# Feed-forward outputs by feature with scale and bias on ScalarE, and two chunk sums on TensorE in every second block

## The chip, the cores and the metric

The kernel runs on one core of a Trainium2 chip. The metric is the device time in microseconds (us), the median of several executions. Five engines work side by side, each through its own queue in program order: TensorE (PE; its weight loads are shown apart as PEld), VectorE (DVE), ScalarE (ACT), GpSimd (POOL) and SyncE (SP), which issues most transfers. TensorE writes its results into PSUM, used here as eight banks of 128 partitions by 512 float32 numbers.

## The reference

```python
# x: (4, 2048, 512); 16 heads of 32; w = sign(weights), +1 or -1
q, k, v = (x @ W.T split into heads for W in (Wq, Wk, Wv))
attn = softmax(q @ k.T / sqrt(32))          # over all 2048 keys
x = layernorm(x + attn @ v)
y = clip((x @ w.T) * scale + bias, -100, 100)   # scale, bias: one per output feature
x = layernorm(x + y)
```

## The kernel before

There are 4 batches. The 16 heads are taken in 4 head groups of 4 heads (`NG = HG = 4`), so there are 16 passes `n` (batch `n // 4`, group `n % 4`). A pass has 4 query blocks `qb` of 512 queries, and a block has 16 key chunks `kc` of 128 keys. A step `s` is one chunk of one block: 64 steps (`STEPS`) to a pass and 1024 in all.

In every step TensorE computes `scores` (L323): four small bf16 matmuls (L327) that add the negated row maxima, then four matmuls of 32 rows each (L333) into four banks. ScalarE turns these into exponentials `p` (L340). `max_unit` (L264) computes scores a second time for a step some 22 ahead, in the other orientation (L275), into four more banks; VectorE takes the row maximum of three of them (L282), ScalarE copies the fourth to SBUF (`moved`, L294) and VectorE reads it there. In every even step `weighted` (L344) multiplies two chunks of `p` with the values (L351), and VectorE adds the result to `oT` (L363). `max_parts` collects a block's maxima once per block.

The sums over `p` are needed as softmax denominators. GpSimd adds the chunks of a block into `acc` (`add_up`, L372, the add is L377); `chunks_added` says how many chunks go there. The chunks from there on are kept in `last_p`, and `denominators` (L400) sums them and `acc` over the keys on TensorE with a matrix of ones (`ones_times`, L381 to L385). `ppool` has five buffers for `p`.

Everything else is put between as tasks: projections of k and q (256 columns each, `project_k`, `project_q`), of v (128 columns, `project_v`), all through `piece` (L229, matmuls L233, ScalarE copy L237), transposes of the input (`transpose_x`, L214), `add_attention` (L460), and the `Finish` of a finished block of rows. A planner (`plan`, L762) decides in which step each goes. A task has a kind ("col", "small" or "big"), a first and a last step, and may wait for another task. In the middle of the program "col" goes into even steps and "small" and "big" into odd steps, one small as a rule and at most two units of big work; `weight` (L759) gives a k or q projection two units. A first plan counts the units of each pass, and the second spreads them by this quota. A step with `add_attention` or with `max_parts` in it is called heavy. Fillers are emitted after the step's scores and row-maximum matmuls and before `weighted`. Calls put into `behind[s]` with `at` are emitted at the end of step `s`.

PSUM banks are handed out by `take` (L83): the bank that a simple model of the engines' times expects free first. `runs`, `spend` and `give` only keep that model. All eight banks are in use by the scores and row maxima of every step.

`Finish` (L481) handles 512 rows of a batch when their attention is complete: `load`, first `stats`, `rstd` (a power on GpSimd, L524), `shift` and `norm` (ScalarE, L542); then per tile `j` of 128 rows `turn` (L548: four transposes L552, `high` on ScalarE L557, the remainder `low` on VectorE L559; both parts are read by matmuls of one pass) and `ffn` (L563) in two halves of 256 output columns. A half is eight matmuls (L570) with a row tile's part as the stationary operand and the sign weights moving, so that rows stand on the partitions, followed by four VectorE operations: times scale (L575), plus bias (L576), clip (L577), all in place in PSUM, and the sum with the row in SBUF (L579). Scale and bias are broadcast to 128 partitions at the start (L180, L181). Then second `stats`, `rstd`, `shift`, `norm` and `store`. `finish` (L611) lays these out for batches 0 to 2, during the passes of the next batch, one block per 64 steps (54 in the last); `finish_last` for the last batch's first three blocks; `finish_end` for its last block, after the last step (`total`), tile by tile.

Of the kernel before, what the change touches and what calls it, by code (L numbers as in the profile page):

```python
# [21 lines left out]
def kernel(  # L22
# [28 lines left out]
    HALF = D // 2  # L51
# [18 lines left out]
    work = ctx.enter_context(tc.tile_pool(name="work", bufs=2))  # L70
# [89 lines left out]
    scale_bc = const.tile([P, D], F32, name="scale_bc")  # L160
    bias_bc = const.tile([P, D], F32, name="bias_bc")

    def load_first():

        first = ppool.tile([P, DC, D], F32, tag="p", name="first_w")
        for i, name in enumerate(("wk", "wq", "wv")):
            xin[name, 0] = first[:, i, :]
        for name in ("wk", "wq"):
            nc.scalar.dma_start(out=xin[name, 0], in_=rows_of[name][ds(0, P), :])
        for g in range(NQB):  # L170
            t = ppool.tile([P, NTQ, D], F32, tag="p", name="first_x")
            for j in range(NTQ):
                xin[0, g, j] = t[:, j, :]
                nc.sync.dma_start(out=t[:, j, :], in_=x[0, ds(g * QB + j * P, P), :])

    def load_rest():
        nc.scalar.dma_start(out=xin["wv", 0], in_=wv[ds(0, P), :])
        raws["ws"] = xpool.tile([P, DC, D], F32, tag="xg", name="raw_ws")
        nc.scalar.dma_start(out=raws["ws"], in_=w_ffn.rearrange("(c p) i -> p c i", p=P))
        nc.sync.dma_start(out=scale_bc, in_=ffn_scale.partition_broadcast(P))  # L180
        nc.sync.dma_start(out=bias_bc, in_=ffn_bias.partition_broadcast(P))  # L181
# [184 lines left out]
    def chunks_added(n, qb):  # L366

        if is_last(n, qb):
            return NT // 2
        return NT - 1  # L370
# [108 lines left out]
    shared = []  # L479

    class Finish:  # L481
        def __init__(self, b, g):
            self.b, self.g = b, g
            self.mv, self.rs, self.nb, self.nT, self.rows_rs = {}, {}, {}, {}, {}
            self.room = None
# [62 lines left out]
        def turn(self, j):  # L548
# [6 lines left out]
            high = work.tile([P, DC, P], F32R, tag="high", name="high")  # L555
            low = work.tile([P, DC, P], F32R, tag="low", name="low")
# [4 lines left out]
            self.nT[j] = high, low  # L561

        def ffn(self, j, half):  # L563
            cols = slice(0, D) if half is None else ts(half, HALF)
            wide = D if half is None else HALF
            i = take()
            py = ps[:, i, :wide]
            for k, part in enumerate(self.nT[j]):
                for c in range(DC):
                    nc.tensor.matmul(  # L570
                        py, lhsT=part[:, c, :], rhs=wT["ws"][:, c, cols],
                        start=(k == c == 0), stop=(k == 1 and c == DC - 1),
                    )
            runs("full", 3.4e-3 * wide)
            nc.vector.tensor_tensor(py, py, scale_bc[:, cols], ALU.mult)  # L575
            nc.vector.tensor_tensor(py, py, bias_bc[:, cols], ALU.add)  # L576
            nc.vector.tensor_scalar(py, py, MAX_VAL, -MAX_VAL, ALU.min, ALU.max)  # L577
            dst = self.row(j)[:, cols]
            nc.vector.tensor_tensor(dst, dst, py, ALU.add)  # L579
            give(i, "DVE", 0.6 + 4.2e-3 * wide)  # L580
# [30 lines left out]
    def finish(b, qb, a, every, w, lag):  # L611
        f = Finish(b, qb)
        at(a, f.load)
        for j in range(NTQ):
            at(a + 2 + j, f.stats, 1, j)
        at(a + 6, f.rstd, 1)
        at(a + 7 + lag, f.shift, 1)
        for j in range(NTQ):
            t = a + 8 + lag + every * j
            at(t, f.norm, 1, j)  # L620
            turned = task("small", t + 1, t + 3, f.turn, j)
            for k in range(2):
                task("big", t + 2, t + w, f.ffn, j, k, after=turned)
            at(t + w, f.stats, 2, j)
        e = a + 9 + lag + every * (NTQ - 1) + w
        at(e, f.rstd, 2)
        at(e + 1 + lag, f.shift, 2)
        for j in range(NTQ):
            at(e + 2 + lag + j, f.norm, 2, j)
        at(e + 5 + lag, f.store)  # L630

    def finish_last(qb, last):
# [9 lines left out]
        for j in range(NTQ):  # L642
            t = a + 5 + (j if late else 3 * j)
            by = t + 6
            at(t, f.norm, 1, j)
            if late:
                by = total + (-1, 1, 4, 5)[j]
            turned = task("small", t + 1, t + 3, f.turn, j)
            for k in [None] if late else range(2):
                task("big", by if late else t + 2, by, f.ffn, j, k, after=turned)  # L650
            at(by + late, f.stats, 2, j)
        e = total + 7 if late else a + 21
# [6 lines left out]
    def finish_end(qb, last):  # L659
# [10 lines left out]
        for j in range(NTQ):  # L670
            t = total + (6, 6, 7, 8)[j]
            turned = task("small", t, t, f.turn, j)
            t = total + 7 + j
            task("big", t, t, f.ffn, j, None, after=turned)
            at(t, f.stats, 2, j)
            at(t, f.rstd, 2, j, j + 1)
            at(t + 1, f.shift, 2, j, j + 1)
            at(t + 1, f.norm, 2, j)
            at(t + 1, f.store_tile, j)
# [16 lines left out]
    for n in range(N):  # L696
# [32 lines left out]
        for qb in range(NQB):  # L729
# [12 lines left out]
            if g == NG - 1:  # L742
                if b < B - 1:
                    every = 13 if b < B - 2 else 11
                    finish(b, qb, (b + 1) * NG * STEPS + qb * (5 * every - 1), every, every, 3)
                else:
                    (finish_end if is_last(n, qb) else finish_last)(qb, last)
# [8 lines left out]
    def on_vector(t):  # L756
        return t[3].__name__ == "ffn"

    def weight(t):  # L759
        return 2 if t[3] in (project_k, project_q) else 1  # L760

    def plan(quota=None):  # L762
# [9 lines left out]
        while any(len(gone[kind]) < len(tasks[kind]) for kind in tasks):  # L772
# [10 lines left out]
            for kind in most:  # L783
# [8 lines left out]
                if kind == "big":  # L792
                    if middle and quota is not None and not heavy:
                        k = max(1, min(k, -(-quota[group] * (at_n + 1) // STEPS) - used[group]))


                    thirds = [t for t in can if on_vector(t)]
                    values = [t for t in can if t[3] is project_v]
                    wide = [t for t in can if weight(t) == 2]
                    if heavy or any(map(on_vector, must)):  # L800
                        thirds = []
                    k -= sum(map(weight, must))
                    if k < 1:
                        can = []
                    elif must:
                        can = values[:1] or thirds[:1]
                    elif k == 1:
                        can = values[:1] or thirds[:1] or wide[:1]
                    elif thirds and values:
                        can = thirds[:1] + values[:1]  # L810
                    else:
                        can = wide[:1] or values[:2] or thirds[:1]
                else:
                    can = can[: max(0, k - len(must))]
                picked = must + can
                for t in sorted(picked, key=lambda t: not on_vector(t)):
# [94 lines left out]
```

## Time and profile before

| | |
|---|---|
| median of 3 runs | 4385.39 us (4384.27 to 4385.4) |
| profiled execution, its time | 4384.56 us |
| profiled execution, its span | 4382.7 us, granted clock 0.996 |
| PE, PEld busy | 4331.6, 2081.3 us |
| DVE, ACT, POOL busy | 3381.3, 2994.6, 4083.0 us |
| chain of work that ended last | PE 94%, DVE 2%, POOL 2%, ACT 2% |

The span runs from the first to the last instruction; the time also holds what lies around it. Busy times overlap, since the engines work side by side. A busy PE can still wait: matmuls are pipelined, and a group of four that starts together and has one member waiting is shown as busy throughout. So for PE the distance from the start of one group to the start of the next says more than its busy time.

### The profile page before, as it was taken

The numbers are of one execution on the slowest core, as the hardware profiler recorded it, in microseconds if no ns is written. First come the engines' busy times: TensorE is split into PE (matmuls) and PEld (weight loads), VectorE is DVE, ScalarE is ACT, GpSimd is POOL, SyncE is SP. The second block draws the span as 40 slices with busy tenths as digits, with TensorE's granted clock in tenths as the row PEclk, the third lists the DMA queues.
The fourth block names the chain that finished last, engine by engine and source line by source line (L and its number), as shares of the span: only waits on it lengthen the run. The fifth ranks groups of instructions, "written<-read, shape, count | busy, mean of one in ns | idle before, by whom it ended". The sixth has DMA issues, their size and how long they took to land.

```text
span 4382.7 us, 88304 instructions
## 1 busy us (share of the span) xinstructions
PE 4331.6 (99%) x35644; PEld 2081.3 (47%) x35644; DVE 3381.3 (77%) x5924; ACT 2994.6 (68%) x6173; POOL 4083.0 (93%) x937
## 2 busy tenths in 40 slices
PE   9999999999999999999999999999999999999997
PEld 5444444444444444445444444444544444444443
DVE  6777777777778777777777877877787777878785
ACT  4666666676667667676676766767666676767675
POOL 4999999999999999999999999999999999999993
PEclk9999999999999999999999999999999999999998
DMA  2000000010001000011000100001100000001101
GB/s 74 11 14 17 11 21 10 16 40 17 21 13 29 11 23 20 11 45 36 21 20 11 33 10 21 23 10 49 28 20 21 20 21 23 20 11 33 24 23 49
DMA packets 259938, 101.60 MB, mean 23 GB/s; under 512 B 168908, under 2 KB 234444, under 8 KB 259528
## 3 DMA queue, kind: packets, MB, share of 16 engines
q1 hardware_dynamic: 258568, 94.12, 8.7%
q8 instruction: 279, 4.57, 0.4%
q10 hardware_dynamic: 960, 1.84, 0.1%
q14 instruction: 131, 1.07, 0.1%
HBM read 54.52 MB, written 33.02 MB: 20 GB/s over the span
## 4 chain that ended last, share of the span: by engine, by line
PE 94%; DVE 2%; POOL 2%; ACT 2%; issue 0%; DMA 0%; ACTq 0%; POOLq 0%; DVEq 0%; SPq 0%
PE ps L275 21%; PE ps L351 21%; PE ps L333 19%; PE ps L233 16%; PE ps L327 8%; PE ps L383 3%; PE ps L570 3%; POOL acc L377 2%; ACT p L340 1%; PE ps L425 1%; PE ps L221 1%; PE ps L552 1%; DVE part L282 1%; DVE st L516 0%; DVE ps L576 0%
## 5 line engine op out<-in xcount | busy, mean ns | idle before, releaser
L377 POOL TENSOR_TENSOR acc<-acc,p 128x2048 f32<-128x2048 f32 x825 | 3744.2, 4538 | 104.1 <-ACT p L340 43.8
L340 ACT ACTIVATE p<-ps 128x512 f32<-128x512 f32 x4096 | 2115.0, 602 | 1148.4 <-PE ps L333 1143.4
L282 DVE TENSOR_REDUCE part<-ps 128x1 f32<-128x512 f32 x3072 | 1933.4, 683 | 660.4 <-PE ps L275 659.8
L275 PE MATMUL ps<-kT,qT 32*128 32x512 f32 x8192 | 1190.5, 592 | 1.9 <-ACT p L340 1.5
L333 PE MATMUL ps<-qT,kT 32*128 32x512 f32 x8192 | 1083.6, 593 | 0.0
L351 PE MATMUL ps<-p,vv 128*32 128x512 f32 x8192 | 984.9, 598 | 1.6 <-DVE low L559 1.0
L275 PEld LDWEIGHTS ps<-kT,qT 32*128 32x128 f32 x8192 | 568.2, 184 | 429.8 <-issue 206.5
L282 DVE TENSOR_REDUCE part<-moved 128x1 f32<-128x512 f32 x1024 | 692.5, 676 | 0.3 <-ACT moved L294 0.3
L294 ACT COPY moved<-ps 128x512 f32<-128x512 f32 x1024 | 631.2, 616 | 20.4 <-PE ps L275 19.7
L351 PEld LDWEIGHTS ps<-p,vv 128*32 128x32 f32 x8192 | 220.3, 109 | 687.4 <-issue 338.4
L327 PE MATMUL ps<-negm,ones_bf 32*128 32x512 bf16 x4096 | 458.2, 384 | 11.6 <-DMA negm<-split 3.9
L333 PEld LDWEIGHTS ps<-qT,kT 32*128 32x128 f32 x8192 | 406.2, 184 | 53.5 <-issue 37.5
L363 DVE TENSOR_TENSOR oT<-ps,oT 128x512 f32<-128x512 f32 x448 | 309.8, 692 | 123.1 <-PE ps L351 81.6
L377 POOL TENSOR_TENSOR acc<-p 128x2048 f32<-128x2048 f32 x64 | 291.0, 4546 | 108.7 <-ACT p L340 108.6
L327 PEld LDWEIGHTS <-ones_bf 32*128 32x128 bf16 x4096 | 106.4, 91 | 558.2 <-issue 521.3
L233 PEld LDWEIGHTS ps<-wvT,xT 128*128 128x128 f32 x2048 | 247.7, 191 | 102.0 <-ACT p L340 96.1
L233 PE MATMUL ps<-wvT,xT 128*128 128x128 f32 x2048 | 283.2, 282 | 0.3 <-ACT p L340 0.3
L233 PE MATMUL ps<-xT,wqT 128*128 128x256 f32 x1024 | 250.6, 388 | 0.0
L233 PE MATMUL ps<-xT,wkT 128*128 128x256 f32 x1024 | 247.2, 387 | 0.2 <-ACT p L340 0.2
L233 PEld LDWEIGHTS ps<-xT,wqT 128*128 128x128 f32 x1024 | 184.1, 189 | 69.2 <-ACT p L340 48.6
L233 PEld LDWEIGHTS ps<-xT,wkT 128*128 128x128 f32 x1024 | 185.3, 190 | 61.3 <-ACT p L340 38.9
L361 DVE COPY oT<-ps 128x512 f32<-128x512 f32 x64 | 44.3, 692 | 131.4 <-PE ps L351 131.4
(76 smaller groups left out, 1755.4 us busy)
## 6 DMA issues: line engine op xcount, KB each, us to landing
xc<-in_L_attn_x_dram SPq DMA_DIRECT2D x60, 256.0 KB
res<-xc SPq DMA_DIRECT2D x60, 256.0 KB
xs<-in_L_attn_x_dram SPq DMA_DIRECT2D x48, 256.0 KB
xg<-res SPq DMA_DIRECT2D x12, 1024.0 KB
out_dram<-xg SPq DMA_DIRECT2D x12, 1024.0 KB
first_x<-in_L_attn_x_dram SPq DMA_DIRECT2D x16, 256.0 KB
xg_last<-res SPq DMA_DIRECT2D x4, 768.0 KB
out_dram<-xg_last SPq DMA_DIRECT2D x3, 1024.0 KB
```

The costliest lines, as they stand in the source:

```text
L233: nc.tensor.matmul(pp, lhsT=lhs(c), rhs=rhs(c), start=(c == 0), stop=(c == DC - 1))
L275: nc.tensor.matmul(ps[:, banks[h], :], lhsT=qT[n, qb][rows, ts(qc, P)], rhs=kT[n][rows, ts(kb, QB)], start=True, stop=True,)
L282: nc.vector.tensor_reduce(part[:, qc, h : h + 1, kb], src, AX.X, ALU.max, negate=True)
L294: nc.scalar.copy(moved, ps[:, banks[-1], :])
L327: nc.tensor.matmul(ps[:, banks[h], :], lhsT=ones_bf[rows, :], rhs=negm[n, qb][rows, :], start=True, stop=False,)
L333: nc.tensor.matmul(ps[:, banks[h], :], lhsT=kT[n][rows, ts(kc, P)], rhs=qT[n, qb][rows, :], start=False, stop=True,)
L340: nc.scalar.activation(p[:, h, :], ps[:, banks[h], :], AF.Exp, scale=SM_SCALE)
L351: nc.tensor.matmul(pb[cols, :], lhsT=vv[n][:, kc, cols], rhs=p[:, h, :], start=(i == 0), stop=(i == 1),)
L363: nc.vector.tensor_tensor(outs[n, qb], pb, outs[n, qb], ALU.add)
L377: nc.gpsimd.tensor_tensor(a, before if kc == 1 else a, p, ALU.add)
L383: nc.tensor.matmul(ps[h * HD : (h + 1) * HD, b, :], lhsT=ones, rhs=p[:, h, :], start=start, stop=stop,)
L570: nc.tensor.matmul(py, lhsT=part[:, c, :], rhs=wT["ws"][:, c, cols], start=(k == c == 0), stop=(k == 1 and c == DC - 1),)
```

## The change

The feed-forward is computed by feature. `turn` writes the parts of two row tiles into one pair of buffers of 256 columns (`work` now has one buffer per tag instead of two). `ffn` takes a pair of tiles and a half: for two blocks `f` of 128 output features, the sign weights are the stationary operand and the 256 rows of the pair move, eight matmuls each into one half of a bank. Features now stand on the partitions, so scale and bias are one number per partition, and ScalarE applies both in one activation per `f`, in place. VectorE clips the whole bank into `yT` in SBUF. A new step, `turn_out`, transposes a tile's four feature blocks back and adds them to the row. Scale and bias are loaded as 128 x 4 numbers and no longer broadcast.

In passes 4 to 15, blocks with an odd `qb` add one chunk less on GpSimd, and `denominators` sums two chunks of `p` beside `acc` (the very last block keeps its own rule). `first_w` takes its buffer from `apool`.

The tasks are laid out again in pairs, in all three finishing functions. The planner counts a feed-forward half as two units, never places it in a heavy step, gives a step that already has a task one v projection alone when few units are due ("light"), and otherwise prefers the wide tasks (k, q, feed-forward) or two v projections.

```diff
-        return NT - 1
+        return NT - 1 if n < NG or qb % 2 == 0 else NT - 2
...
-            high = work.tile([P, DC, P], F32R, tag="high", name="high")
-            low = work.tile([P, DC, P], F32R, tag="low", name="low")
+            if j % 2 == 0:
+                self.parts = [
+                    work.tile([P, DC, 2 * P], F32R, tag=part, name=part) for part in ("high", "low")
+                ]
+            high, low = (part[:, :, ts(j % 2, P)] for part in self.parts)
...
-            nc.vector.tensor_tensor(py, py, scale_bc[:, cols], ALU.mult)
-            nc.vector.tensor_tensor(py, py, bias_bc[:, cols], ALU.add)
-            nc.vector.tensor_scalar(py, py, MAX_VAL, -MAX_VAL, ALU.min, ALU.max)
-            dst = self.row(j)[:, cols]
-            nc.vector.tensor_tensor(dst, dst, py, ALU.add)
-            give(i, "DVE", 0.6 + 4.2e-3 * wide)
+        def ffn(self, pair, half):
+
+            if half == 0:
+                self.yT = work.tile([P, DC, 2 * P], F32, tag="yT", name="yT")
             i = take()
+            py = cols_of(i, 2, 2 * P)
+            for f in range(2):
+                for k, part in enumerate(self.parts):
+                    for c in range(DC):
+                        nc.tensor.matmul(
+                            py[:, f, :], lhsT=wT["ws"][:, c, ts(2 * half + f, P)],
+                            rhs=part[:, c, :],
+                            start=(k == c == 0), stop=(k == 1 and c == DC - 1),
+                        )
+            runs("full", 1.9)
+            for f in range(2):
+                oc = slice(2 * half + f, 2 * half + f + 1)
+                nc.scalar.activation(
+                    py[:, f, :], py[:, f, :], AF.Identity,
+                    bias=bias_t[:, oc], scale=scale_t[:, oc],
+                )
+            spend("ACT", 0.75, clock["PE"] + 0.2)
+            nc.vector.tensor_scalar(
+                self.yT[:, 2 * half : 2 * half + 2, :], py, MAX_VAL, -MAX_VAL, ALU.min, ALU.max
+            )
+            give(i, "DVE", 0.7)
+
+        def turn_out(self, j):
+
+            i = take()
+            pt = cols_of(i, DC, P)
+            for c in range(DC):
+                nc.tensor.transpose(pt[:, c, :], self.yT[:, c, ts(j % 2, P)], ident)
+            runs("full", 0.44)
+            nc.vector.tensor_tensor(self.row(j), self.row(j), ps[:, i, :], ALU.add)
+            give(i, "DVE", 0.7)
...
+    def pair(f, i, turn, ffn, back):
+
+        for k in range(2):
+            t = task("small", *turn[k], f.turn, 2 * i + k, after=halves[0])
+        for k in range(2):
+            t = task("big", *ffn[k], f.ffn, i, k, after=t)
+        halves[0] = t
+        for k in range(2):
+            task("small", *back[k], f.turn_out, 2 * i + k, after=t)
+            at(back[k][1] + 1, f.stats, 2, 2 * i + k)
...
+            t = a + 11 + every * i
+            at(t, f.norm, 1, 2 * i)
+            at(t + 2, f.norm, 1, 2 * i + 1)
+            z = t + every
+            pair(f, i, [(t + 1, t + 5), (t + 3, t + 7)], [(t + 4, z - 10), (t + 4, z - 8)],
+                 [(t + 6, z - 4), (t + 6, z - 2)])
...
-                    every = 13 if b < B - 2 else 11
-                    finish(b, qb, (b + 1) * NG * STEPS + qb * (5 * every - 1), every, every, 3)
+                    every, apart = (26, STEPS) if b < B - 2 else (22, 54)
+                    finish(b, qb, (b + 1) * NG * STEPS + qb * apart, every)
...
-        return 2 if t[3] in (project_k, project_q) else 1
+        return 2 if t[3] in (project_k, project_q) or t[3].__name__ == "ffn" else 1
...
+                    if heavy:
+                        wide = [t for t in wide if t[3].__name__ != "ffn"]
                     k -= sum(map(weight, must))
+                    light = steps[s] and values and not heavy and due < 2.5
                     if k < 1:
                         can = []
-                    elif must:
-                        can = values[:1] or thirds[:1]
-                    elif k == 1:
-                        can = values[:1] or thirds[:1] or wide[:1]
-                    elif thirds and values:
-                        can = thirds[:1] + values[:1]
+                    elif must or k == 1:
+                        can = values[:1] or ([] if must else wide[:1])
+                    elif light or due < 1.25 and not heavy:
+                        can = values[:1] or wide[:1]
                     else:
-                        can = wide[:1] or values[:2] or thirds[:1]
+                        can = wide[:1] or values[:2]
```

Here `due` is the pass's quota of units up to this step less those already placed.

## The prediction

> **What bounds the kernel now.** I read the page's busy shares first, then GpSimd's timeline (its adds mark the blocks: sixteen chunks of one head group's 512 queries), then busy time by stretch, and last single steps in the timeline.
>
> ```profile
> PE 4331.6 (99%) x35644; PEld 2081.3 (47%) x35644; DVE 3381.3 (77%) x5924; ACT 2994.6 (68%) x6173; POOL 4083.0 (93%) x937
> ```
>
> Two engines look full, TensorE and GpSimd. Which one sets the pace differs by batch:
>
> ```profile
> 411.44 4.55 POOL L377 TENSOR_TENSOR acc<-p 128x2048 f32<-128x2048 f32 x1 [0.76 <-ACT p L340]
> 416.07 59.88 POOL L377 TENSOR_TENSOR acc<-acc,p 128x2048 f32<-128x2048 f32 x13
> 475.91 4.56 POOL L377 TENSOR_TENSOR acc<-p 128x2048 f32<-128x2048 f32 x1
> ...
> 1384.92 4.55 POOL L377 TENSOR_TENSOR acc<-p 128x2048 f32<-128x2048 f32 x1
> ...
> 1517.54 4.54 POOL L377 TENSOR_TENSOR acc<-p 128x2048 f32<-128x2048 f32 x1 [1.60 <-ACT p L340]
> ...
> 1651.98 4.54 POOL L377 TENSOR_TENSOR acc<-p 128x2048 f32<-128x2048 f32 x1
> ```
>
> In the first batch (no feed-forward yet) GpSimd's adds follow one another without a gap: 14 adds of 4.6 us are 64.5 us, and that is the block (411.44 to 475.91). From the second batch on, four blocks take 267.1 us (1384.92 to 1651.98), GpSimd needs 4 x 64.5 + 2 x 1.0 (its two powers) = 260, and it waits for ScalarE's exponentials in most blocks. There GpSimd is not the bound.
>
> ```profile
> 411.40:669.40 258.00, 257.17 (x2164) 120.27 (x2164) 192.31 (x323) 176.87 (x364) 253.89 (x57) 1.00 0.07 15
> 1384.90:1652.00 267.10, 267.10 (x2210) 127.64 (x2209) 211.36 (x373) 184.31 (x381) 256.06 (x60) 1.00 0.08 19
> ```
>
> The columns are length, then PE, PEld, DVE, ACT, POOL. "PE busy" hides waits inside it, so I go by the distance from one group of matmuls to the next. A clean row-maximum group (L275) lasts 0.96 us to its successor. One feed-forward half (L570) stretches the next one:
>
> ```profile
> 1459.17 0.73 PE L570 MATMUL ps<-wsT,high 128*128 128x256 f32 x4
> 1459.27 1.89 DVE L282 TENSOR_REDUCE part<-ps 128x1 f32<-128x512 f32 x3 [0.65 <-PE ps L275]
> ...
> 1460.22 1.05 PE L233 MATMUL ps<-wvT,xT 128*128 128x128 f32 x8
> ...
> 1461.08 0.42 DVE L575 TENSOR_TENSOR ps<-ps,scale_bc 128x256 f32<-128x256 f32 x1
> ...
> 1462.29 1.77 PE L275 MATMUL ps<-kT,qT 32*128 32x512 f32 x8
> ...
> 1462.47 0.42 DVE L579 TENSOR_TENSOR xg<-xg,ps 128x256 f32<-128x256 f32 x1
> ...
> 1462.94 0.29 PEld L275 LDWEIGHTS ps<-kT,qT 32*128 32x128 f32 x2 [0.46 <-DVE xg L579]
> ...
> 1463.99 0.64 PE L351 MATMUL ps<-p,vv 128*32 128x512 f32 x4
> ```
>
> L275 starts at 1462.29 and its successor at 1463.99: 1.70 us, 0.74 lost. Scores and row maxima take four PSUM banks each, all eight, so the next row-maximum group cannot start its last matmul before the slowest bank of the step before is free; here that is the feed-forward's, held by four VectorE operations of 0.42 to 0.43 us that queue behind three row maxima. A turn beside one v projection loses likewise, 1545.33 to 1546.89, 0.60 over:
>
> ```profile
> 1545.33 1.62 PE L275 MATMUL ps<-kT,qT 32*128 32x512 f32 x8
> ...
> 1545.83 0.30 PEld L275 LDWEIGHTS ps<-kT,qT 32*128 32x128 f32 x4 [0.31 <-DVE low L559]
> ...
> 1546.89 1.06 PE L351 MATMUL ps<-p,vv 128*32 128x512 f32 x8
> ```
>
> Over four such blocks the L275 distances add up to 70.3 us; four early first-batch blocks have 4 x 15.7 = 62.8. So 7.5 us of 267 are these waits: about 8 x 0.75 for halves and 2 x 0.6 for turns. That is all the change can win per four blocks.
>
> **The change, part by part** (four blocks hold one Finish: four 128-row tiles, two pairs).
>
> *Matmuls of the feed-forward.* Before: 4 tiles x 2 halves x 8 of 256 columns; after: 2 pairs x 2 halves x 16 of 256. Same number, same width; sixteen in a row take 2.1 us (merged entry of the chain). Zero.
>
> *Turning back (turn_out).* Four more transposes per tile. The same four in turn (L552) take 0.49 us to their successor, 0.43 without the switch that a following v then no longer pays: 4 x 0.43 = +1.7. The Trainium skill speaks for more ("TensorE: Matmul & The Clock Gate", Part 4: about 275 ns per transpose inside a kernel, so 1.1 us per tile): that would be 4.4, or 30 us more over eleven groups. The row is of the same shape in the same step, so I take it. Below zero it cannot be: all are added.
>
> *Two chunks on TensorE.* In odd blocks of later batches, 23 in all, GpSimd's 14th add (4.54 us) becomes four more ones-matmuls. That group (L383, one chunk) takes 0.88 us to its successor: +1.75 per four blocks. It frees GpSimd 9.2 us per four blocks, which buys nothing where GpSimd already waits. Were it the bound it would buy up to 260 - 251; the waits above exclude that.
>
> *Waits behind the feed-forward.* After: matmuls 2.1, two ScalarE activations, one VectorE clip. Durations: a 256-column copy from PSUM is 0.37 us (L237); a pointer operand adds about 0.09 (L535 with a pointer scale 284 ns, L531 without 193), and both scale and bias are pointers: 0.56; the second in a row adds 0.46 (four L535 in a row overlap by 0.09 each): 1.02. Clip 0.70 (L577 at 512 columns). With hops of 0.1 and 0.03 the bank is free 1.85 us after the last matmul, while the scores between take 1.09: the next row-maximum group loses 0.76, plus 0.1 for its weight loads: 0.86. The choice here is when the first activation starts. No row shows an engine reading a bank into which TensorE still writes: every reader in the trace starts after the bank's last matmul. The skill's "PSUM — Partial Sum Buffer" ("PSUM bank collisions raise a hardware error") says that two engines may not touch one bank and quadrant at once, even at different columns. By it both activations wait for all sixteen matmuls (0.86); by the data alone the first would hide under the last eight (bank free 1.3 us after the end, loss about 0.4). I take 0.86, and 0.4 as the low end: 4 x 0.86 = 3.4.
>
> *Waits behind turns.* The planner's new rule gives a step that already has a small task one v projection alone ("light"). By hand, for a group with a pair at steps 11 and 37, all four turns then stand beside a single v: 4 x 0.58 = 2.3, where before two of four stood beside a wide projection and lost nothing. turn_out's add (0.69) follows the row maxima and frees its bank 0.12 after the next group could start: 0.2 twice, 0.3 once where the maxima are collected: 0.7.
>
> *Sum per four blocks:* waits 3.4 + 2.3 + 0.7 = 6.4 against 7.5 (-1.1), turning back +1.7, ones +1.75: +2.3, or +2.2 averaged over the groups with input transposes. Eleven groups (4.0 to 15.0): +24.
>
> *Costed at nothing.* VectorE loses 2.0 us per tile (8 x 0.43 for 2 x 0.69), ScalarE gains about 1.0; both have over 50 us free in 267, and only their order against the banks counts. Without that cover ScalarE's extra would be 4 us per four blocks. Two 256 KB broadcast loads become 2 KB loads in 4-byte pieces on the SP queue near 11 us; behind them is the load of weight rows not turned before the first block; at worst a few us of queue there. Input weights landing in another pool, and single work buffers: a pair's turns wait for the previous pair's matmuls, many steps earlier except at the end. The first batch stays on GpSimd's 64.5.
>
> *Last head group and end.* 4065.1 to 4331.2 is short of TensorE work and pinned by VectorE latency and GpSimd: one add less (4.6) and lighter VectorE, I take -4. After it, from the first cast (4351.23) to the last normalisation (4374.5) are 23 us in four overlapping tiles. As two pairs that share one buffer the chain is: cast and low 1.8, matmuls 4.2, activations and clip 1.7, turn out 1.0, then turns 1.0, cast and low 1.9, 4.2, 1.7, 1.0, adds 1.4, statistics to normalisation 3.3, hops 3: 26. +3. Together -1, within -12 to +10.
>
> The profiled execution has a span of 4382.7 and a time of 4384.56; the median of the runs is 0.8 higher. 4384.6 + 24 - 1 = 4407.6; with the 0.8, 4408.
>
> **The rivals.** *Faster: the waits go.* If turns land beside wide projections and the activations start early, waits fall to 4 x 0.3 + 0.5 = 1.7: -5.8 + 3.45 = -2.4 per four blocks, -26, and -4 at the end: 4355. For it: VectorE is 79% busy in these stretches and is relieved. Against it: the release is a latency, not a load. *About the same: only the first activation hides.* Waits 4.6, +0.5 per four blocks, +6, end -3: 4388. *Much slower: ScalarE comes late.* Activations, a cast and a normalisation (0.84) in adjacent steps delay the exponentials, whose first bank the next filler needs; it decides once ScalarE has over 4.2 us in one step (2.07 + 0.62 + 1.02 + 0.84 is 4.55, in a few steps). At +2.5 per four blocks on top: 4435.
>
> **How the numbers follow.** Forecast (4408, itself 4392 to 4425) 0.46; waits go 0.22; only the first hides 0.20; ScalarE late 0.12. A difference of 0.2%, 8.8 us, is about what a measurement here can tell. Faster by that: nearly all of the second and a little of the third, 0.23; within: most of the third and the low edge of the forecast, 0.19; slower: 0.58. The range 4352 to 4430 leaves out the lower half of "waits go" and most of "late".
>
> **What would show it.** Right: blocks near 67.3 us from the second batch on against 66.8; L275 distances near 69 per four blocks, with 1.8 us after each half; first activation starting after the sixteenth matmul; turns and v together; GpSimd idle about 15 us more per four blocks; first batch unchanged at 64.5. Wrong: activations starting between the eighth and sixteenth matmul, L275 back to 0.96 after halves, blocks under 66.5, or an end longer or shorter by over 10 us.

## The result, and the profile after

The changed kernel takes 4433.3 us (median; 4431.6 to 4435.0), the kernel before 4385.4: a ratio of 1.0109, with a 95% interval from 1.0097 to 1.0121. The forecast was 4408 with a range up to 4430; slower was right, the size was +48 in place of +23. The profiled executions are 4382.7 and 4429.8 us long, 47.1 apart; the table below adds up to that.

The busy shares on the page of the changed kernel:

```profile
PE 4364.8 (99%) x36148; PEld 2095.5 (47%) x36148; DVE 3261.8 (74%) x5572; ACT 3057.8 (69%) x6301; POOL 3979.3 (90%) x914
```

VectorE lost 120 us of work and GpSimd 104, and neither shortened anything: TensorE is as full as before and has 504 instructions more. The timeline of GpSimd shows where the blocks begin (an add without a sum on its input side starts a block):

```profile
411.22 4.55 POOL L376 TENSOR_TENSOR acc<-p 128x2048 f32<-128x2048 f32 x1 [0.73 <-ACT p L339]
...
475.71 4.57 POOL L376 TENSOR_TENSOR acc<-p 128x2048 f32<-128x2048 f32 x1
...
1387.01 4.55 POOL L376 TENSOR_TENSOR acc<-p 128x2048 f32<-128x2048 f32 x1 [5.39 <-ACT p L339]
...
1521.59 4.54 POOL L376 TENSOR_TENSOR acc<-p 128x2048 f32<-128x2048 f32 x1 [7.68 <-ACT p L339]
...
1657.31 4.54 POOL L376 TENSOR_TENSOR acc<-p 128x2048 f32<-128x2048 f32 x1 [5.41 <-ACT p L339]
```

The first batch is as it was (411.22 to 475.71 is 64.5 us). Four later blocks go from 267.1 to 270.3 us (1387.01 to 1657.31), and GpSimd stands idle for 5 to 9 us behind every block in which it has one add less. Busy time by stretch (length, then PE, PEld, DVE, ACT, POOL) says the same:

```profile
411.40:669.40 258.00, 257.05 (x2161) 120.06 (x2160) 192.16 (x323) 176.87 (x364) 253.93 (x57) 1.00 0.07 15
1384.90:1655.30 270.40, 269.33 (x2244) 127.70 (x2240) 203.91 (x349) 188.26 (x389) 247.10 (x56) 1.00 0.08 19
```

Cut at the first exponential of each pass of a head group (four blocks, below: a group), the 47 us lie like this:

| stretch | before | after | difference | forecast |
|---|---|---|---|---|
| start and first batch (4 groups) | 1111.3 | 1110.6 | -0.7 | 0 |
| passes 4 to 14 (11 groups) | 2953.8 | 2987.8 | +34.0 | +24 |
| last head group | 266.1 | 270.5 | +4.4 | -4 |
| after the last exponential | 51.5 | 60.8 | +9.3 | +3 |

Now single steps of the changed kernel. First one feed-forward half (L571), its two activations (L579), its clip (L584) and the row maxima behind it (L274):

```profile
1480.14 0.62 ACT L293 COPY moved<-ps 128x512 f32<-128x512 f32 x1
...
1480.45 0.64 PE L571 MATMUL ps<-low,wsT 128*128 128x256 f32 x4
...
1481.03 0.39 PE L326 MATMUL ps<-negm,ones_bf 32*128 32x512 bf16 x4
...
1481.19 1.11 ACT L579 ACTIVATE ps<-ps,bias_t,scale_t 128x256 f32<-128x256 f32 x2 [0.44 <-PE ps L571]
...
1482.11 2.09 PE L274 MATMUL ps<-kT,qT 32*128 32x512 f32 x8
...
1482.34 0.69 DVE L584 TENSOR_SCALAR yT<-ps 128x512 f32<-128x512 f32 x1 [1.44 <-ACT ps L579]
...
1483.08 0.29 PEld L274 LDWEIGHTS ps<-kT,qT 32*128 32x128 f32 x2 [0.77 <-DVE yT L584]
...
1484.13 0.16 PEld L350 LDWEIGHTS ps<-p,vv 128*32 128x32 f32 x8 [0.76 <-ACT p L339]
```

ScalarE is free at 1480.76, and the first output block has all its eight matmuls by then, but the first activation starts at 1481.19, after the sixteenth. The bank comes free with the clip at 1483.03, the last row-maximum matmul waits for it, and L274 stands from 1482.11 to 1484.13: 2.02 us against 0.96, a loss of 1.06. A turn beside one v projection:

```profile
1435.77 0.66 PE L549 MATMUL ps<-ident,xg 128*128 128x128 f32 x4
...
1438.38 1.63 PE L274 MATMUL ps<-kT,qT 32*128 32x512 f32 x8
...
1438.88 0.30 PEld L274 LDWEIGHTS ps<-kT,qT 32*128 32x128 f32 x4 [0.31 <-DVE low L559]
...
1439.94 1.50 PE L350 MATMUL ps<-p,vv 128*32 128x512 f32 x12
```

1.56 us in place of 0.96, as the forecast had it. The third place was in no term of the forecast. It comes once in each of the eleven groups, and a twelfth time in the last head group (4208.44), in the step where the last tile's second statistics (L513, L514) and the variance step (L519) are issued together; the kernel before issued the variance step one step later than the statistics:

```profile
1646.40 1.03 PE L274 MATMUL ps<-kT,qT 32*128 32x512 f32 x8
1646.72 0.68 DVE L513 BATCH_NORM_STATS2 st<-xg 128x6 f32<-128x512 f32 x1
1647.44 0.18 DVE L514 BATCH_NORM_AGGREGATE mv<-st 128x2 f32<-128x6 f32 x1
...
1647.65 0.30 ACT L519 ACTIVATE ve<-mv,eps_t 128x4 f32<-128x4 f32 x1 [2.35 <-DVE mv L514]
1647.86 2.04 ACT L339 ACTIVATE p<-ps 128x512 f32<-128x512 f32 x4
...
1648.49 1.16 PE L232 MATMUL ps<-wvT,xT 128*128 128x128 f32 x8 [1.06 <-ACT p L339]
```

ScalarE waits 2.35 us for a 0.18 us operation of VectorE. The four exponentials behind it in its queue are ready but cannot pass it; the bank that the next projection takes is one of theirs, and TensorE stands idle for 1.06 us. Last the end, where the last half's matmuls run up to 4409.85:

```profile
4409.20 0.64 PE L571 MATMUL ps<-low,wsT 128*128 128x256 f32 x4
...
4410.65 0.29 ACT L519 ACTIVATE ve<-mv,eps_t 128x1 f32<-128x1 f32 x1 [0.84 <-DVE mv L514]
...
4412.19 0.81 ACT L539 ACTIVATE xg_last<-xg_last,nb,rs 128x512 f32<-128x512 f32 x1
...
4413.46 0.81 ACT L539 ACTIVATE xg_last<-xg_last,nb,rs 128x512 f32<-128x512 f32 x1
4414.18 1.09 ACT L579 ACTIVATE ps<-ps,bias_t,scale_t 128x256 f32<-128x256 f32 x2
```

Its activations start 4.3 us later, behind the first pair's normalisation (L519 to L539) in ScalarE's queue.

### The profile page after: what moved, and what is told of

It reads as the page before. It is cut to its first block, busy times and chain, and to the rows that moved or that the text cites. A ratio compares the mean times of both kernels' runs of the same rounds, so it can differ in the third digit from the quotient of the medians.

```text
span 4429.8 us, 88985 instructions
## 1 busy us (share of the span) xinstructions
PE 4364.8 (99%) x36148; PEld 2095.5 (47%) x36148; DVE 3261.8 (74%) x5572; ACT 3057.8 (69%) x6301; POOL 3979.3 (90%) x914
## 3 DMA queue, kind: packets, MB, share of 16 engines
q14 instruction: 129, 1.06, 0.1%
## 4 chain that ended last, share of the span: by engine, by line
PE 92%; POOL 3%; DVE 2%; ACT 2%; issue 0%; DMA 0%; ACTq 0%; POOLq 0%; DVEq 0%; SPq 0%
PE ps L274 21%; PE ps L350 20%; PE ps L332 19%; PE ps L232 16%; PE ps L326 7%; POOL acc L376 3%; PE ps L382 3%; PE ps L571 3%; ACT p L339 1%; DVE part L281 1%; PE ps L424 1%; PE ps L220 1%; PE ps L594 1%; PE ps L549 1%; DVE st L513 0%
## 5 line engine op out<-in xcount | busy, mean ns | idle before, releaser
L376 POOL TENSOR_TENSOR acc<-acc,p 128x2048 f32<-128x2048 f32 x802 | 3640.3, 4539 | 102.9 <-ACT p L339 44.3
L274 PE MATMUL ps<-kT,qT 32*128 32x512 f32 x8192 | 1185.0, 592 | 1.9 <-ACT p L339 1.9
L332 PE MATMUL ps<-qT,kT 32*128 32x512 f32 x8192 | 1070.2, 591 | 0.0
L350 PE MATMUL ps<-p,vv 128*32 128x512 f32 x8192 | 986.4, 599 | 0.2
L274 PEld LDWEIGHTS ps<-kT,qT 32*128 32x128 f32 x8192 | 552.2, 185 | 446.8 <-issue 242.7
L350 PEld LDWEIGHTS ps<-p,vv 128*32 128x32 f32 x8192 | 220.8, 109 | 685.9 <-issue 337.3
L326 PE MATMUL ps<-negm,ones_bf 32*128 32x512 bf16 x4096 | 437.7, 384 | 9.6 <-DMA negm<-split 3.9
L332 PEld LDWEIGHTS ps<-qT,kT 32*128 32x128 f32 x8192 | 406.3, 184 | 38.4 <-issue 21.0
L326 PEld LDWEIGHTS <-ones_bf 32*128 32x128 bf16 x4096 | 106.5, 91 | 559.2 <-issue 523.8
```

The source lines that it names most:

```text
L274: nc.tensor.matmul(ps[:, banks[h], :], lhsT=qT[n, qb][rows, ts(qc, P)], rhs=kT[n][rows, ts(kb, QB)], start=True, stop=True,)
L326: nc.tensor.matmul(ps[:, banks[h], :], lhsT=ones_bf[rows, :], rhs=negm[n, qb][rows, :], start=True, stop=False,)
L332: nc.tensor.matmul(ps[:, banks[h], :], lhsT=kT[n][rows, ts(kc, P)], rhs=qT[n, qb][rows, :], start=False, stop=True,)
L350: nc.tensor.matmul(pb[cols, :], lhsT=vv[n][:, kc, cols], rhs=p[:, h, :], start=(i == 0), stop=(i == 1),)
L376: nc.gpsimd.tensor_tensor(a, before if kc == 1 else a, p, ALU.add)
```

## The experiments

The theory: the 34 us in the middle are ones-matmuls and turning back, which nothing hides, plus three waits: the output blocks' shared bank, the variance step's wait in ScalarE's queue, and turns beside a single v. The rivals are named with each run. All differences are against the medians of 4433.3 (changed) and of the kernel before in the same runs (4385.8 to 4386.0).

**The second chunk back on GpSimd**, everything else as changed.

```diff
-        return NT - 1 if n < NG or qb % 2 == 0 else NT - 2
+        return NT - 1
```

> The changed kernel with GpSimd adding fourteen chunks in every block again; everything else of the change stays. Theory A (the chunk moved to TensorE is pure cost, since GpSimd waits for exponentials from the second batch on): each of the 23 odd blocks gives back one group of four ones-matmuls, 0.88 us, 23 x 0.88 = 20: 4433 - 20 = 4413, within 4409 to 4417; passes 4 to 14 fall from 270.3 to 268.5. Theory B (GpSimd needs the relief, an odd block being 14 x 4.6 = 64.5 us of its adds plus powers in 66.4): GpSimd comes late, and 4428 to 4440.

Measured: 4412.1 (4410.6 to 4415.0), 21 us less; the eleven middle groups 2970.0, 17.8 less.

**The chunk shift alone, in the kernel before.** The same line, the other way round.

> The kernel before with one part of the change alone: in every second block of later batches TensorE sums two chunks by ones-matmuls and GpSimd thirteen. Theory A (pure cost): 23 groups of four ones-matmuls more, 0.88 us each: 4385 + 20 = 4405, within 4400 to 4409. Theory B (it relieves GpSimd, 93% busy, and lets the exponentials run ahead): 4370 to 4387.

Measured: 4407.9 (4406.5 to 4408.1), ratio 1.0049 (1.0036 to 1.0062): 22 us more, the eleven groups 18.2 more. Both ways round the chunk on TensorE is pure cost, of the forecast's size: 21 odd blocks in these groups by 0.88 is 18.5. GpSimd's 93% was never the limit there.

**The variance step one step later.**

```diff
-        at(z - 1, f.rstd, 2)
-        at(z + 3, f.shift, 2)
+        at(z, f.rstd, 2)
+        at(z + 4, f.shift, 2)
```

with the normalisations and the store behind it moved by one step too.

> The changed kernel with the second normalisation's variance step (ScalarE's ve, GpSimd's power, and what follows them) one step later, so that it no longer stands in the step of the last tile's statistics. Theory A: ScalarE's queue was held by ve until VectorE's mv was there, and the exponentials behind it kept a bank from a projection: 1.13 + 0.14 us once in each of eleven passes, so 4433 - 13 = 4420, within 4416 to 4424, and in the trace the ve of four tiles starts without a gap. Rival: the wait only changes its place (the power and the shift meet the next pass's work): 4430 to 4435.

Measured: 4417.0 (4416.8 to 4417.8), 16 us less; the eleven groups 12.5 less, the last head group 3.6 less (266.9). The variance step in the waits of ScalarE (total, times, longest), in the kernel before, the changed kernel and this one:

```profile
ACT ve L522 <- DVE mv L517: 26.8, 11, 6.1
```

```profile
ACT ve L519 <- DVE mv L514: 42.3, 20, 5.4
```

```profile
ACT ve L519 <- DVE mv L514: 11.1, 9, 5.4
```

Of the waits of the kernel before one lies in the eleven groups, of 0.91 us; of the changed kernel's, eleven lie there, and a twelfth of 4.47 us in the last head group. One step later these twelve are gone and one of 0.69 us is new: 31 us less of ScalarE's idle time, of which TensorE had felt 12.5 in the eleven groups.

**A bank for each output block.** A half takes two banks, and each block is clipped by itself.

```diff
-            py = cols_of(i, 2, 2 * P)
+            banks = [take(), take()]
+            py = [ps[:, i, : 2 * P] for i in banks]
...
-            nc.vector.tensor_scalar(
-                self.yT[:, 2 * half : 2 * half + 2, :], py, MAX_VAL, -MAX_VAL, ALU.min, ALU.max
-            )
-            give(i, "DVE", 0.7)
+            for f in range(2):
+                nc.vector.tensor_scalar(
+                    self.yT[:, 2 * half + f, :], py[f], MAX_VAL, -MAX_VAL, ALU.min, ALU.max
+                )
+                give(banks[f], "DVE", 0.42)
```

> The changed kernel with each of the two output blocks of a feed-forward half in a PSUM bank of its own, and one clip of 256 columns for each in place of one of 512. Theory A (the first activation waits for all sixteen matmuls because they share its bank): ScalarE is free 0.4 us before the sixteenth matmul ends, so the first activation starts there and the second follows; the wait behind a half falls from 1.06 to about 0.25, 44 halves x 0.8 = 35: 4433 - 35 = 4398, within 4390 to 4408. Rival B (the chain of activation, clip and queue sets the wait, not the shared bank): the loss stays near 0.9, 4424 to 4432. Rival C (the second bank is missed by the row maxima): slower than 4436.

Measured: 4389.2 (4385.8 to 4391.0), 44 us less, and level with the kernel before (ratio 1.0005, 0.9997 to 1.0013). The timeline of one half:

```profile
1460.52 0.64 PE L571 MATMUL ps<-low,wsT 128*128 128x256 f32 x4
1460.62 1.18 ACT L579 ACTIVATE ps<-ps,bias_t,scale_t 128x256 f32<-128x256 f32 x2
...
1461.24 0.42 DVE L584 TENSOR_SCALAR yT<-ps 128x256 f32<-128x256 f32 x1 [0.27 <-ACT ps L579]
...
1461.83 0.42 DVE L584 TENSOR_SCALAR yT<-ps 128x256 f32<-128x256 f32 x1 [0.16 <-ACT ps L579]
...
1462.17 1.25 PE L274 MATMUL ps<-kT,qT 32*128 32x512 f32 x8
...
1463.36 1.07 PE L350 MATMUL ps<-p,vv 128*32 128x512 f32 x8
```

The first activation starts while the second block's last matmuls still run, and the first clip beside the second activation. L274 stands for 1.19 us: 0.23 lost in place of 1.06. Four halves by 0.83 are 3.3 us a group; the eleven groups fell by 3.5 each on average (2949.5 together).

**One bank, two clips.** The two banks had also brought a split clip; this run has the split alone.

```diff
-            nc.vector.tensor_scalar(
-                self.yT[:, 2 * half : 2 * half + 2, :], py, MAX_VAL, -MAX_VAL, ALU.min, ALU.max
-            )
+            for f in range(2):
+                nc.vector.tensor_scalar(
+                    self.yT[:, 2 * half + f, :], py[:, f, :], MAX_VAL, -MAX_VAL, ALU.min, ALU.max
+                )
```

> The changed kernel with the clip of a feed-forward half split in two of 256 columns, both output blocks still in one bank. It takes the split clip away from what two banks brought. Theory A (the shared bank holds the first activation back): the first activation still starts after the sixteenth matmul, the first clip hides beside the second activation, and the wait behind a half falls from 1.06 by 0.27 (a clip of 0.69 against one of 0.42): 44 x 0.27 = 12, 4433 - 12 = 4421, within 4416 to 4430. Theory B (the split clip was what brought it): 4388 to 4402.

Measured: 4435.2 (4433.8 to 4438.1), no gain, so theory B is out; but my number was wrong too. The timeline says why:

```profile
1482.34 0.39 PE L326 MATMUL ps<-negm,ones_bf 32*128 32x512 bf16 x4
...
1482.51 1.11 ACT L579 ACTIVATE ps<-ps,bias_t,scale_t 128x256 f32<-128x256 f32 x2 [0.43 <-PE ps L571]
...
1483.65 0.76 DVE L585 TENSOR_SCALAR yT<-ps 128x256 f32<-128x256 f32 x2 [1.44 <-ACT ps L579]
```

The shared bank keeps VectorE out as well: the first clip has its data at about 1483.05 (0.54 for an activation), yet starts only after the second activation, at 1483.65. In these runs TensorE, ScalarE and VectorE take turns at one bank, and splitting the work paid only with separate banks. (Whether the chip or the semaphores that the program was built with enforce this, these runs do not tell apart.)

**No lone v beside a small task.**

```diff
-                    light = steps[s] and values and not heavy and due < 2.5
+                    light = False
```

> The changed kernel without the planner's new rule that gives a step with a small task (a turn, a turning back, an input transpose) one v projection alone. Theory A (a turn beside a single v loses 0.60 us because the next row maxima come 0.9 us sooner than beside a wide projection): the four losses of 0.60 in a pass go, and about two small ones of 0.35 come with v projections that now stand elsewhere: 11 x 1.7 = 19, 4433 - 19 = 4414, within 4407 to 4424. Rival (the wide projections taken from other steps leave losses of the same size there): 4429 to 4437.

Measured: 4429.9 (4429.6 to 4432.5), 3.5 us less, which is hardly clear of the spread of the runs (4431.6 to 4435.0 changed); the rival is nearer. In the head group of pass 5 two of the four turns no longer cost their 0.60, but v projections now stand alone in three more steps, and the scores behind them (L326, L332) lose 0.2 to 0.3 each: 270.3 became 270.1. The waits that the forecast priced at 4 x 0.58 are there, but without the planner's rule most of it is lost elsewhere.

**Another order at the end.**

```diff
-                pair(f, i, [(s + 2, s + 2), (s + 2, s + 2)], [(s + 4, s + 4), (s + 5, s + 5)],
+                pair(f, i, [(s + 2, s + 2), (s + 2, s + 2)], [(s + 3, s + 3), (s + 3, s + 3)],
...
+            t += 5 - i
             for j in (2 * i, 2 * i + 1):
-                at(t + 4, f.rstd, 2, j, j + 1)
+                at(t, f.rstd, 2, j, j + 1)
```

(shift, normalisation and store of the last group's pairs in the same way; the late group's first pair is turned back in one step.)

> The changed kernel with another order of issue after the last scores: the second pair of the late group runs its feed-forward halves one and two steps earlier, and the first pair of the last group is normalised behind the second pair's last activations. Same operations, same buffers. Theory A (at the end the activations stand in ScalarE's queue behind normalisations: the last half's matmuls end at 4409.85 and its activations start at 4414.18): the end shortens by 3 to 6 us, 4427 to 4430. Rival (the single buffer of a pair and the length of the chain set the end): no change, 4432 to 4435.

Measured: 4433.6 (4429.2 to 4434.5), no change, and the part after the last exponential 60.2 against 60.8. The last half's activations now follow their matmuls without a queue, but the variance steps of the last two tiles come late in their turn, though their statistics are done at 4420.34:

```profile
4414.81 1.11 ACT L579 ACTIVATE ps<-ps,bias_t,scale_t 128x256 f32<-128x256 f32 x2
...
4419.60 2.22 ACT L539 ACTIVATE xg_last<-xg_last,nb,rs 128x512 f32<-128x512 f32 x3
...
4421.73 0.46 ACT L519 ACTIVATE ve<-mv,eps_t 128x1 f32<-128x1 f32 x2
```

This order did not shorten the end. I read it as the same sum of ScalarE's work in the same chain, where whatever is put first delays the rest; no run here shows that. (Each of the late pair's halves came one step earlier, the second not two: no step took two halves.)

**The last batch tile by tile.** The four groups of the last batch with the kernel before's turn, feed-forward (scale, bias, clip and addition on VectorE) and schedule; the first of a tile's two halves is due two steps sooner, and the scale and bias rows use the input rows' buffers.

```diff
-                pair(f, i, [(t + 1, t + 5), (t + 2, t + 6)], [(t + 4, t + 9), (t + 4, t + 11)],
-                     [(t + 6, t + 13), (t + 6, t + 15)])
...
+            turned = task("small", t + 1, t + 3, f.turn_row, j)
+            for k in [None] if late else range(2):
+                task("big", by if late else t + 2, by if late or k else by - 2, f.ffn_row, j, k, after=turned)
```

> The changed kernel with the last batch's four groups finished tile by tile as before (a tile's rows in the output's partitions, scale, bias, clip and addition on VectorE, no turning back); batches 0 to 2 stay changed. Theory A (in the last pass and at the end the pair-wise form costs 4 and 9 us, since its activations add to ScalarE's serial chain of casts and normalisations, and tiles no longer overlap): the last pass near 266, the end near 52, 4433 - 14 = 4419, within 4413 to 4425. Rival (the last pass and the end are longer for other reasons, such as the one chunk more on TensorE or where the blocks stand): 4428 to 4436.

Measured: 4424.2 (4421.3 to 4428.6), 9 us less. After the last exponential it takes 52.6 us (60.8 changed, 51.5 before): that part is the pair-wise form's. The last head group did not follow: 274.0. But this profile is of the slowest of the five executions, and TensorE's clock was at half for 20.5 us of that group (10.2 in the changed kernel; see the last section), so the run does not settle the last head group.

**Everything mended at once**: no second chunk, later variance step, two banks, last batch tile by tile.

> The changed kernel with four things mended at once: no chunk on TensorE beyond the one before, the second variance step one step later, a bank for each output block of a half, and the last batch finished tile by tile. If the gains add (21, 16, 44, and 14 expected of the last): 4433 - 95 = 4338. Theory A with a bound: a pass of four blocks comes to 270.3 - 1.7 - 1.2 - 3.6 = 263.8, while GpSimd's adds and powers take 260, so part is lost: 4338 to 4352. Theory B (with the waits gone GpSimd is the bound, and the chunk on TensorE would have been needed): passes of 266 or more, above 4365.

Measured: 4347.3 (4346.5 to 4348.5), 0.9912 of before (0.9898 to 0.9925). The head group of pass 5 takes 264.0 us, as added up, and over the eleven groups the gains of the single runs add up too: 17.8, 12.5 and 38.3 are 68.6, and 69.2 are measured. Of the sum over the whole (21, 16, 44 and 9 are 90) 4 us are missing, outside of these groups.

**The same with the second chunk on TensorE kept.**

> The combined kernel (a bank for each output block, later variance step, last batch tile by tile) with the change's second chunk on TensorE kept. Theory A (pure cost also where a pass is down to 264 us): 4347 + 21 = 4368, within 4362 to 4373. Theory B (at 264 us a pass GpSimd, with 260 us of adds and powers, is nearly the bound, so the relief pays for part of the ones-matmuls): 4347 to 4358.

Measured: 4369.1 (4366.8 to 4369.6): 22 us more, 18.3 of them in the eleven groups. Even where a group takes 264 us and GpSimd has 260 us to do, relieving it is worth nothing.

**The combined kernel without the rule of one v.**

> The combined kernel without the planner's rule of one v projection alone beside a small task. Theory A: as in the changed kernel, 11 x 1.7 = 19 less, if GpSimd allows it (260 us of adds and powers in a pass of 264): 4347 - 19 = 4328, within 4325 to 4340. Theory B (GpSimd is now the bound, and what TensorE gains it waits again): 4342 to 4348.

Measured: 4344.8 (4344.2 to 4345.3), ratio 0.9905 (0.9890 to 0.9920), the fastest of all. It is 2.5 us under the combined kernel, not the 19 that I expected; as in the changed kernel the projections lose elsewhere what the turns win, so this is no evidence for GpSimd as the bound (theory B named that range for another reason).

## Why the prediction was right or wrong

- *Slower, because GpSimd is not the bound.* Right, and shown three times (removed, added alone, added to the combined kernel): 17.8, 18.2 and 18.3 us for the 21 odd blocks of the eleven groups, 0.85 to 0.87 each where 0.88 was costed. One of the signs does not follow from the forecast's own terms: "about 15 us more" idle time of GpSimd would be 9.2 freed and 2.3 of longer blocks, 11.5. The rows give 12.3 (23.3 against 11.0).
- *Turning back, +1.7 a group.* In the head group of pass 5 the four groups L594 take 1.97 us together: 0.49 each, the row's full length, not the 0.43 taken. The page "TensorE: Matmul & The Clock Gate" (the Trainium skill, Part 4) names about 275 ns for a bf16 transpose in one kernel, and a single float32 one in this trace does last 273 ns; but within a group they start 0.11 us apart and overlap, so adding up whole durations, to 4.4 us, is too much. Taking the row was right.
- *Both activations wait for all sixteen matmuls.* Right, in the trace and by the two-bank run. That choice rested on the Trainium skill, "PSUM — Partial Sum Buffer" ("PSUM bank collisions raise a hardware error"), and the rows agree, between ScalarE and VectorE too (1483.65 above). With the low end (0.4 a half) the sum would have been 20 us lower than taken.
- *The size of that wait.* 1.06 a half in place of 0.86: the bank came free 1.94 us after the last matmul, not 1.85 (two activations 1.11, not 1.02), and the row maxima started 1.02 after it, not 1.09. Four halves: +0.8 a group.
- *Turns beside a single v, 0.58.* 0.60, four times a group, at the steps worked out. But reading them as the price of the planner's rule would be wrong: without the rule the kernel gains 3.5 us, not 26.
- *The step that failed: "only their order against the banks counts".* ScalarE's and VectorE's work was costed at nothing because both have 50 us free. The order that mattered was inside ScalarE's own queue: with the new schedule the second variance step falls into the step of the last statistics, ScalarE waits there 2.35 us and more for VectorE, and ready exponentials stand behind it. One step later the kernel takes 16 us less: 12.5 in the eleven groups (1.1 each) and 3.6 in the last head group. It is the largest single term of the 25 us that the forecast missed. The rival "ScalarE comes late" had the right place (late exponentials hold a filler's bank) but the wrong mechanism: it asked for over 4.2 us of ScalarE work in one step and +2.5 a group, and what came was a wait on VectorE. That its time, 4435, is nearly the measured one is luck; much of the rest lies at the end.
- *A gain that was missed.* The forecast counted the waits of the kernel before at L275 alone and took them for all that can be won. In pass 5 eight more steps of it, with one v projection alone, lose 0.20 each between the scores' L327 and L275; in the changed kernel one such step is left. L326 and L332 take 1.5 us less in this group, 14.5 over the eleven. So the balance of pass 5 is +1.97 turning back, +1.72 ones, +1.2 at L274, -1.5, and -0.2 in other fillers: +3.2, against +2.2 forecast. That the eleven groups came out only 10 us above the forecast is partly luck: the variance step (12.5) and the larger waits behind halves (9) were missed on one side, these 14.5 on the other.
- *End +3.* +9.3, of which tile by tile takes 8.2 back. The forecast's chain of 26 us counted one pair after another, with activations that start when their matmuls end; the trace has the late pair's activations, four casts and the normalisations in one ScalarE queue. Reordering did not help. Shown is that the pair-wise form costs it; that ScalarE's larger share of the chain is the reason is read from the timelines only, and how much the single buffer of a pair adds was not tried.
- *Last head group -4.* +4.4, and settled in part only. The twelfth wait of the variance step stands in it, with 1.89 us of TensorE's idle time behind it; one step later the group takes 266.9 in place of 270.5. The chunk shift alone moved it from 266.1 to 270.6, and taking it out from 270.5 to 267.0, more than two groups of 0.88. By the clock records of the traces the group is at half clock for 3.4 us before, 10.2 changed, 13.7 with the chunk shift alone and 6.8 with the later variance step, so part of these differences is the clock (see below); how much was not separated. The forecast's gain of 4.6 from one add less is not there in any run.

## What to carry to other kernels

Before moving work off a busy engine, ask which wait ends last in the stretch: 93% busy was not a bound, and the relief cost its full price on the engine that was. Results that different engines read one after another belong in separate PSUM banks when TensorE comes round again for the same bank: here the second bank was worth 44 us of 4433, and splitting the readers without it nothing. And when a schedule is rewritten by hand, look on each in-order queue for an operation issued in the same step as the one it waits for: it holds everything behind it.

## What the hardware showed that I had not expected

The last head group, with long waits on TensorE, differs by 2.6 us (270.5 and 273.1) between two profiles of the same instructions. The run with another order at the end has the changed kernel's instructions up to the last exponential. In both, TensorE stands idle behind the twelfth variance step; in the changed kernel:

```profile
4208.44 0.48 ACT L519 ACTIVATE ve<-mv,eps_t 128x4 f32<-128x4 f32 x2 [4.47 <-DVE mv L514]
...
4209.46 0.69 PE L274 MATMUL ps<-kT,qT 32*128 32x512 f32 x1 [1.89 <-ACT p L339]
```

The stretches behind this stall (length, PE, PEld, DVE, ACT, POOL, then the granted TensorE clock), first in the changed kernel:

```profile
4210.00:4214.00 4.00, 3.91 (x21) 1.79 (x19) 0.86 (x2) 2.26 (x5) 4.00 (x4) 0.58 0.01 4
4214.00:4218.00 4.00, 4.00 (x37) 1.49 (x38) 2.97 (x5) 2.57 (x9) 3.92 (x2) 0.99 0.00 0
```

and then in the reordered one:

```profile
4210.00:4214.00 4.00, 4.00 (x17) 2.38 (x20) 1.33 (x3) 2.37 (x5) 4.00 (x4) 0.50 0.02 4
4214.00:4218.00 4.00, 4.00 (x21) 0.99 (x18) 1.89 (x3) 3.16 (x10) 4.00 (x1) 0.50 0.00 0
4218.00:4222.00 4.00, 4.00 (x33) 1.28 (x26) 1.28 (x2) 0.82 (x2) 3.92 (x2) 0.74 0.00 0
```

After the stall TensorE is granted half its clock, in one profile for some 3.4 us and in the other for some 10; the next group of weighted sums (L350) takes 1.85 us in the first, where the clock is full again, and 3.57 in the second. So the same wait of 2 us can cost more in one execution than in another. In the run with the later variance step this stall is gone, and the clock stays at 1.00 there:

```profile
4193.00:4197.00 4.00, 3.88 (x32) 2.13 (x30) 3.96 (x9) 2.73 (x6) 3.92 (x2) 1.00 0.00 0
```

The Trainium skill ("TensorE: Matmul & The Clock Gate", Part 1) describes the half clock after a window of idleness of some 3.4 us that runs freely. The clock records of both traces agree with the window: up to the last exponential each stretch at half clock is 3.41 us long or a whole multiple of it (10.24 in the reordered run), and the starts lie whole multiples of 3.41 us apart. But an idle time of 1.89 us was enough here. The waits of 1.06 us in the middle of the kernel did not do it (granted clock 1.00 over the group from 1384.90 on), nor did one of 1.74 us in the first batch of the changed kernel (at 861).
